# Four transformer blocks in one launch: when the first sequence's value products of attentions 1 and 3 may run

## The chip, the cores and the metric

The kernel runs on one core of a Trainium2 chip. The core has a matrix engine (PE; its weight loads are listed apart as PEld), a vector engine (DVE), a scalar engine (ACT), a general engine (POOL) and an engine that issues transfers (SP). Each engine works through its own list of instructions in the order in which the program wrote them, and waits for the others at semaphores. The metric is the time of one execution on the device in microseconds (us); the quoted time is a median of runs.

## The reference

`reference()` passes `x` (4 sequences of 512 tokens, 288 channels, float32) through four blocks. Each block takes a conditioning vector per sequence, makes six rows of shift, scale and gate from it, and adds an attention and a feed-forward part to `x`:

```
mod = silu(c) @ w_ada + b_ada                       # shift, scale, gate, twice
h   = layernorm(x) * (1 + scale) + shift
q, k, v = split(h @ w_qkv + b_qkv)                  # 16 heads of 18
x   = x + gate * (softmax(q k^T / sqrt(18)) v @ w_proj + b_proj)
h   = layernorm(x) * (1 + scale2) + shift2
x   = x + gate2 * feed_forward(h)                   # 288 -> 1152 -> 288, gelu
```

Blocks 0, 1 and 3 attend over the tokens of a sequence. Block 2 attends, for each token, over its own 16 heads. The feed-forward part of block 0 is a mixture of four experts, two for each token; the other blocks have one plain feed-forward part.

## The kernel before

**Stages.** On the PE, attention 0 comes first, then the experts (19 blocks of 256 rows, `expert_block`), then attention 1. Attention 2 (`attention_over_heads`, a generator called the chain) runs beside the feed-forward part of block 1 and the beginning of that of block 2, whose remainder (`half_mlp`) is followed by attention 3 and its feed-forward part.

**Attention over tokens** (`attention`, called for blocks 0, 1, 3). The work is cut into 16 units: four sequences times four groups of four heads. A unit has four steps, one for each 128 tokens, so there are 64 steps. A step computes two things for the four heads of a unit: in `weights` the scores of its 128 keys and the exponentials of them (ACT, line 750), and in `maxima` the scores of 128 queries of the unit six steps ahead, whose row maxima DVE takes (line 722). `sum_values` multiplies the exponentials with the values, two steps at a time.

**What a unit needs.** `queries_keys(b, m)` computes a packed block of 128 rows of queries and keys (line 640; ACT copies it out at line 666). `spread(u)` then moves the rows of unit `u` by nine transfers (line 702) to their places in a tile `qk`: for each head `j` the queries or keys go to the partitions `32 j` and up, in pieces of at most 19 rows. The first unit of attention 1 sends heads 0 and 1 by SP and heads 2 and 3 by ACT; the first unit of attention 3 sends heads 0 and 1 by SP and heads 2 and 3 by POOL. `values(b, t)` computes the values of 128 tokens: three matrix products (line 640, six records of 288 columns each) and a DVE copy into the tile `va` (line 650).

**Before step 0.** Attentions 1 and 3 are "hidden": the maxima that belong to the steps −6 to −1 are made by `ahead(step, c)` while the PE still works on the feed-forward part before. One `ahead` makes the scores of four heads in two pairs, heads 0 and 1 and then heads 2 and 3 (line 712), and DVE reduces each (line 735). `set_maxima(0)` then turns the maxima of the first unit.

**The order of the work** is fixed when the program is written. The feed-forward functions call `gap(us)` between small groups of matrix products. A gap raises a counter `now` by one and takes work out of the list `products`, which is sorted by due time: the first task in the list whose keys are all marked as ready is taken, **due or not**, as long as the gap's budget is above 0 (0.5 in the experts, 0.3 in `half_mlp`). A value product costs 0.48 for each of its three products, a pair of `ahead` 1.3. After the products, the gap gives the lists of DVE work, of loads and of spreads their turn. `spread` marks its unit as ready two gaps after it was written. So the order rests on a count of gaps; when the data really arrives is a matter of the semaphores alone: an engine that reaches an instruction too early stands still.

While attention 2's chain is alive, a gap closes whatever task it took, that is, it writes it out whole. If a step of the chain wants a bank of PSUM and the gap's products used one, the chain waits for the next gap; in that next gap `products` gets a budget of 0, and the chain comes first.

In the steps, `whole_products(us)` plays the part of the gap: it raises the counter twice, takes ready tasks until their cost passes the budget (0.3 in even steps, 1.7 in odd ones), and beyond it takes those that are due. Even steps put products in the banks 0 to 3, odd ones in 4 to 7, beginning at the first; these are the banks that the scores of the step use too.

The value products are entered so, `s0` being 0 for the first sequence:

```
for t in range(TB):
    free = ("va", l) if b == 0 else ("values free", l, b - 1, t)
    at = s0 + (-1, -1, 1 if b else 0, 1)[t]
    hold = [("step", l, at)] if at >= 0 else [] if l else [("step", l, -2)]
    task(
        products, start - 30 if at < first_step else at_step(at),
        [("ht", l, 0, b), ("loaded", l, 0), free] + hold, values(b, t)
    )
```

A task with `hold` can't be taken before its step is marked. Other due times ahead of step 0 are −50, −48 and −34 for the packed blocks 0 to 2, −20 for block 3, and −24, −21, ... −9 for the six `ahead`.

Of the kernel before, what the change touches and what calls it, by code (L numbers as in the profile page):

```python
# [60 lines left out]
def tile_dit_blocks(ctx: ExitStack, tc: tile.TileContext, x_in, cond_t, sel_den, sel_b, w_gate, layers, out):  # L61
# [52 lines left out]
    def task(where, due, reads, gen):  # L114
        where.append((due, reads, gen))
        where.sort(key=lambda item: item[0])
# [449 lines left out]
    def chunks(l, half, b):  # L566

        key = (l, half, b)
        mod = mods[l, half]
        if half == 0:  # L570
            ht[key] = work.tile([P, NK, S], F32, tag="ht", bufs=2, name=f"ht_{l}_{half}_{b}")
        else:
            ht[key] = work.tile([P, NK, S], F32, tag="hm", bufs=4, name=f"ht_{l}_{half}_{b}")
        for k in range(NK):
            if half == 0:
                at, n = k * KP, KP + (1 if k == NK - 1 else 0)
            else:
                at, n = k * P, P if k < KF else CX - KF * P
            to = other()
            for t in range(TB):  # L580
                nc.tensor.transpose(to[:n, t * P : (t + 1) * P], xh[key][:, t, at : at + n], ident)
            nc.scalar.activation(
                ht[key][:n, k, :], to[:n, :], AF.Identity, bias=mod[:n, 0, k, b : b + 1],
                scale=mod[:n, 1, k, b : b + 1],
            )
            if k == NK - 1:
                held.remove(key)
                mark(("ht",) + key)
            yield Whole(0.43)
# [15 lines left out]
    def attention(l, start):  # L605
# [14 lines left out]
        def at_step(s):  # L620
            return start + 2 * (s - first_step) + 1
# [22 lines left out]
        def values(b, t):  # L644
            pv = other()[:, :C]
            h = ht[l, 0, b]
            yield from product(
                pv, lambda r, k: h[r, k, t * P : (t + 1) * P], lambda r, k: w["wv"][r, k, :], 0.48
            )
            nc.vector.tensor_copy(heads(vas[0])[:, t, :, :HD], pv.rearrange("p (h d) -> p h d", d=HD))  # L650
            mark(("values", l, b, t), 0)
            count(b)
            yield 0.48
# [17 lines left out]
        def straight(u):  # L671

            h, t = ht[l, 0, 0], spreads_of[u]
            qk[u] = t
            for s in range(2):
                pq = other()
                yield from product(pq, lambda r, k: wholes[0][r, u, k, s, :], lambda r, k: h[r, k, :], 0.86)
                nc.scalar.activation(t[:, s, :], pq, AF.Copy)
                count(0)
                if s:  # L680
                    mark(("spread", l, u), 1)
                    if u == direct[-1]:
                        warm = small.tile([P, 1], F32, tag="warm", bufs=1, name=f"warm_{l}")
                        nc.scalar.activation(warm, ident[:, :1], AF.Exp)
                yield Whole(0.86)
# [139 lines left out]
        def project(b, t):  # L825
            pp = other()[:, :C]
            for k in range(NK):
                n = KP + (1 if k == NK - 1 else 0)
                nc.tensor.matmul(  # L829
                    pp, done["turned", b, k][:n, t * P : (t + 1) * P], w["wp"][:n, k, :], start=k == 0, stop=k == NK - 1  # L830
                )
                if k < NK - 1:
                    yield 0.48
            add_gated(b * TB + t, 1, pp.unsqueeze(1), gates[l, 0], f"a_{l}_{b}_{t}")
            if t == TB - 1:
                mark(("x", l, 1, b))
            yield 0.48
# [60 lines left out]
        def ring_of(b, m):  # L898

            m, b = (m - 3, b) if m >= 3 else (m - 3 + NQB, b - 1)  # L900
            if b < 0:
                return None
            return b * NG + min(NG - 1, ((m + 1) * P - 1) // UQ)
# [13 lines left out]
        for b in range(B):  # L917
            s0 = b * NG * TB
            last = s0 + NG * TB
            first = hidden and b == 0  # L920
            task(
                lanes, start - 70 if first else at_step(s0 - LEAD - (9 if l or b > 1 else 12) if b else s0 - LEAD - 6),
                [("x", l, 0, b)] + ([("scattered", B - 1)] if l == 1 else []) + ([("step", l, 0)] if b else []),
                norm(l, 0, b, 10 if first and prev == OVER_HEADS else 3),
            )
            free = [("first products", l, b - 2)] if b >= 2 else []
            if prev == OVER_HEADS and b < 2:

                free = [[("first products", prev, B - 1), ("x", prev, 1, B - 2)], [("x", prev, 1, B - 1), ("first products", l, 0)]][b]
            task(  # L930
                products, start - 60 if first else at_step(s0 - 12 if b else s0 - LEAD - 4),
                [("xh", l, 0, b), ("mod", l, 0)] + free, chunks(l, 0, b),
            )
            for t in range(TB):
                free = ("va", l) if b == 0 else ("values free", l, b - 1, t)
                at = s0 + (-1, -1, 1 if b else 0, 1)[t]
                hold = [("step", l, at)] if at >= 0 else [] if l else [("step", l, -2)]
                task(
                    products, start - 30 if at < first_step else at_step(at),
                    [("ht", l, 0, b), ("loaded", l, 0), free] + hold, values(b, t)  # L940
                )
                at = last + (3, 4, 6, 8)[t] if b + 2 < B else last + (3, 5, 7, 9)[t]
                hold = [("step", l, at)] if b + 1 < B else []
                task(
                    products, at_step(last if b + 1 == B else at),
                    [("turned", l, b, k) for k in range(NK)] + [("gate", l, 0), ("projection", l)] + hold,
                    project(b, t),
                )
            for u in direct if b == 0 else ():
                task(  # L950
                    products, at_step(-LEAD - 2 + 4 * u),
                    [("ht", l, 0, 0), ("whole", l, u)] + ([("step", l, -LEAD)] if u else []), straight(u),
                )
            for m in range(2 if b == 0 and direct else 0, NQB):
                free = [("spread", l, ring_of(b, m))] if ring_of(b, m) is not None else idle
                at = s0 + (((-10, -9, -5, -1, 3) if l else (0, 0, -4, -3, 3)) if b == 0 else (-11, -9, -7, -5, -3))[m]
                hold = [("step", l, at)] if at >= 0 or l == 0 else []
                due = start - (50, 48, 34, 20)[m] if hidden and at < 0 else at_step(at)
                units = range(m * P // UQ, min(NG, -(-(m + 1) * P // UQ)))
                task(  # L960
                    products, due, [("ht", l, 0, b)] + [("loaded", l, g) for g in units] + free + hold,
                    queries_keys(b, m),
                )
            for g in range(NG):
                u, s = b * NG + g, s0 + g * TB
                free = [("qk free", l, u - 4)] if u >= 4 else idle
                blocks = range(g * UQ // P, -(-(g + 1) * UQ // P))
                if u not in direct:
                    task(
                        spreads, start - (42, 32)[u] if hidden and u < 2 else at_step(s - LEAD - 2),  # L970
                        [("packed", l, b, m) for m in blocks] + free + ["cleared"] + ([("set", l, 0)] if direct and u == 2 else []),
                        spread(u),
                    )
                due = start - 9 if hidden and u == 0 else at_step(s + 1 - LEAD + TB - 2) + 1
                task(products, due, [("maxima", l, u)], set_maxima(u))
                at = s + TB + (2 if g < NG - 1 else 1)
                hold = [("step", l, at)] if at < N_STEPS - LEAD else []
                task(products, at_step(at), [("sums", l, u)] + hold, outputs(u))
            for k in range(NK):
                at = s0 + (12, 16, 18)[k]  # L980
                hold = [("step", l, at)] if at < N_STEPS - LEAD else []
                task(products, at_step(at), [("outputs", l, b * NG + g) for g in (k, k + 1)] + hold, turned(b, k))
# [1035 lines left out]
    for l in range(n_layers):  # L2018
# [7 lines left out]
        if l == 0:  # L2026
# [4 lines left out]
            for i, half in enumerate(halves):  # L2031
                free = [("step", 0, 7 * i + 1)] + ([("modulated",) + halves[i - 1]] if i else [])
                at = base + 2 * (LEAD + 7 * i) + 2
# [190 lines left out]
```

## Time and profile before

| | us |
|---|---|
| median of 3 runs (2169.55 to 2182.09) | 2180.47 |
| the profiled execution, its own time | 2180.11 |
| its span, from the first to the last instruction | 2178.4 |
| PE busy | 2056.8 (94%) |
| DVE busy | 1067.0 (49%) |
| ACT busy | 813.6 (37%) |
| POOL busy | 541.3 (25%) |
| mean granted PE clock | 0.975 |
| stages on the PE: step 0 of attention 1 begins at | 836.26 |
| step 0 of attention 3 begins at | 1695.85 |

Times inside the execution count from the start of the span. In a timeline, a line gives the start, the length, the engine (with a q where it issues a transfer), the line of the kernel, the operation, the tiles written and read, their shapes, the number of instructions merged, and in brackets how long the engine had stood idle and who released it. A float32 matrix product appears as two records. The ends of PE records are modelled, so the distance between starts is the better measure. In a table of stretches, each line gives the stretch, its length, the busy time of PE, PEld, DVE, ACT and POOL with the number of instructions, the granted PE clock, the share of the transfer engines and GB/s.

### The profile page before, as it was taken

The numbers are of one execution on the slowest core, as the hardware profiler recorded it, in microseconds if no ns is written. First come the engines' busy times: TensorE is split into PE (matmuls) and PEld (weight loads), VectorE is DVE, ScalarE is ACT, GpSimd is POOL, SyncE is SP. The second block draws the span as 40 slices with busy tenths as digits, with TensorE's granted clock in tenths as the row PEclk, the third lists the DMA queues.
The fourth block names the chain that finished last, engine by engine and source line by source line (L and its number), as shares of the span: only waits on it lengthen the run. The fifth ranks groups of instructions, "written<-read, shape, count | busy, mean of one in ns | idle before, by whom it ended". The sixth has DMA issues, their size and how long they took to land.

```text
span 2178.4 us, 28974 instructions
## 1 busy us (share of the span) xinstructions
PE 2056.8 (94%) x10782; PEld 1156.8 (53%) x10782; DVE 1067.0 (49%) x1656; ACT 813.6 (37%) x1333; POOL 541.3 (25%) x589
## 2 busy tenths in 40 slices
PE   7899999899999998999999999979999999999997
PEld 3334434367777574344354667656767444443554
DVE  4656656532002404576445769699730555664101
ACT  2434444522222123445436332333422555455211
POOL 2212131231004112020011395769711101001101
PEclk9999999999999999999999999979999999999999
DMA  4153222346666353000000000302210100000000
GB/s 95 54 178 119 61 59 37 109 148 195 203 200 199 113 170 93 21 26 17 19 6 20 18 9 16 69 17 30 34 50 18 40 19 18 14 18 1 11 11 22
DMA packets 171832, 139.13 MB, mean 64 GB/s; under 512 B 80694, under 2 KB 153838, under 8 KB 171692
## 3 DMA queue, kind: packets, MB, share of 16 engines
q1 hardware_dynamic: 163370, 123.92, 20.3%
q0 software_dynamic: 8224, 13.20, 2.1%
q8 instruction: 86, 1.41, 0.3%
q14 instruction: 54, 0.44, 0.1%
q10 hardware_dynamic: 98, 0.16, 0.0%
HBM read 96.49 MB, written 26.00 MB: 56 GB/s over the span
## 4 chain that ended last, share of the span: by engine, by line
PE 65%; DVE 14%; POOL 3%; issue 2%; ACT 2%; DMA 1%; SPq 0%; POOLq 0%; DVEq 0%; ACTq 0%
PE banks L712 12%; PE banks L640 8%; PE banks L1739 7%; PE banks L1719 6%; PE banks L778 5%; PE banks L1893 4%; PE banks L1870 4%; PE banks L1952 3%; DVE pq L1021 3%; PE banks L1930 3%; DVE hs L1027 3%; DVE mx L722 3%; PE banks L829 3%; PE banks L1725 2%; POOL pv L1040 1%
## 5 line engine op out<-in xcount | busy, mean ns | idle before, releaser
L722 DVE TENSOR_REDUCE mx<-banks 128x4 f32<-128x2048 f32 (+1 forms) x354 | 423.7, 1238 | 352.7 <-PE banks L712 319.3
L750 ACT ACTIVATE ex<-banks 128x1024 f32<-128x1024 f32 (+1 forms) x471 | 377.6, 865 | 312.1 <-PE banks L712 312.0
L712 PE MATMUL banks<-qk 32*128 32x512 f32 x3072 | 440.4, 627 | 26.6 <-DVE mx L722 7.4
L712 PEld LDWEIGHTS banks<-qk 32*128 32x128 f32 x3072 | 167.8, 185 | 201.3 <-issue 73.1
L1040 POOL TENSOR_TENSOR pv<-hs,qk 128x1152 f32<-128x1152 f32 x60 | 192.5, 3233 | 9.8 <-ACT hs L1194 9.8
L778 PE MATMUL banks<-ex,va 128*32 128x512 f32 x1536 | 191.6, 612 | 2.5 <-ACT ex L750 2.5
L640 PE MATMUL banks<-ht,wqk 96*128 96x512 f32 (+1 forms) x348 | 169.2, 619 | 10.2 <-DVE mx L722 9.7
L1739 PE MATMUL banks<-w_b,hid_b 128*128 128x288 f32 x648 | 175.3, 416 | 0.0
L1719 PE MATMUL banks<-block,w_b 128*128 128x256 f32 (+1 forms) x684 | 159.0, 371 | 0.6 <-ACT hid_b L1731 0.6
L1930 PE MATMUL banks<-ht,w 128*128 128x256 f32 x504 | 133.1, 400 | 21.3 <-ACT hid L1941 21.2
L1952 PE MATMUL banks<-w,hid 128*128 128x288 f32 x504 | 147.5, 429 | 0.0
L1739 PEld LDWEIGHTS banks<-w_b,hid_b 128*128 128x128 f32 x648 | 117.9, 189 | 51.0 <-issue 22.1
L1731 ACT ACTIVATE hid_b<-banks,b_b 128x256 f32<-128x256 f32 (+1 forms) x171 | 66.8, 461 | 198.4 <-PE banks L1725 128.6
L1719 PEld LDWEIGHTS banks<-block,w_b 128*128 128x128 f32 x684 | 122.7, 191 | 26.6 <-issue 8.9
L764 POOL DMA_DIRECT2D qk<-maxima x48 | 29.8, 620 | 381.4 <-ACT maxima L763 381.3
L1930 PEld LDWEIGHTS banks<-ht,w 128*128 128x128 f32 x504 | 98.1, 200 | 44.6 <-ACT hid L1941 24.9
L599 POOL TENSOR_TENSOR x<-x,upd_a 128x288 f32<-128x288 f32 x48 | 38.6, 805 | 315.0 <-DVE upd_a L598 288.5
L640 PEld LDWEIGHTS banks<-ht,wqk 96*128 96x128 f32 (+1 forms) x348 | 61.4, 187 | 102.8 <-issue 57.2
L1952 PEld LDWEIGHTS banks<-w,hid 128*128 128x128 f32 x504 | 91.5, 194 | 45.6 <-issue 26.2
L778 PEld LDWEIGHTS banks<-ex,va 128*32 128x32 f32 x1536 | 40.2, 110 | 139.5 <-issue 71.2
L1941 ACT ACTIVATE hid<-banks,b 128x256 f32<-128x256 f32 x126 | 53.6, 471 | 136.9 <-PE banks L1937 136.8
L1052 DVE TENSOR_REDUCE ho<-pv 128x72 f32<-128x1152 f32 x64 | 85.2, 1337 | 30.6 <-POOL pv L1040 30.6
(244 smaller groups left out, 2458.1 us busy)
## 6 DMA issues: line engine op xcount, KB each, us to landing
w_b<-in_w SPq DMA_DIRECT2D x57, 432.0 KB
w_b<-in_w SPq DMA_DIRECT2D x57, 384.0 KB
qk<-qc SPq DMA_DIRECT2D x270, 38.0 KB
wa<-in_wada SPq DMA_DIRECT2D x24, 288.0 KB
x_mem<-zeros SPq DMA_DIRECT2D x21, 256.0 KB
y_mem<-zeros SPq DMA_DIRECT2D x21, 256.0 KB
block<-x_mem SPq DMA_DIRECT2D x17, 288.0 KB
y_mem<-y_b SPq DMA_DIRECT2D x17, 288.0 KB
```

The source lines that it names most:

```text
L640: nc.tensor.matmul(to, st(rows, k), mv(rows, k), start=k == 0, stop=k == NK - 1)
L712: nc.tensor.matmul(to, qk[u][r, of, c * P : (c + 1) * P], qk[u][r, 1 - of, :], start=True, stop=True)
L722: nc.vector.tensor_reduce(mxs[u % 2][:, j : j + n, c], banks[:, bank + j : bank + j + n, :], AX.X, ALU.max)
L750: nc.scalar.activation(ex[step, j // 2][:, j % 2 : j % 2 + n, :], banks[:, to[j] : to[j] + n, :], AF.Exp, scale=SCALE)
L778: nc.tensor.matmul(to[j * HP : (j + 1) * HP, :], vas[0][:, c, at : at + HP], ex[step, j // 2][:, j % 2, :], start=first, stop=last,)
L1040: engine.tensor_tensor(prod, sc[i][:, hs, :].unsqueeze(2).to_broadcast([P, GH, HD, NH]), qkv[i, 2].rearrange("p h d -> p d h").unsqueeze(1 ...
L1719: nc.tensor.matmul(banks[:, UP + j, cols], w1[:, k, j * P : (j + 1) * P], hx[i][:, k, cols], start=k == 0, stop=False)
L1739: nc.tensor.matmul(banks[:, PY + t, :C], hid[j][:, t * P : (t + 1) * P], w2[:, j, :], start=f == 0, stop=f == NF - 1)
L1870: nc.tensor.matmul(banks[:, 4 + j, :], full[:, k, (f % 3) * P : (f % 3 + 1) * P], h[:, k, :], start=k == 0, stop=False,)
L1893: nc.tensor.matmul(banks[:, t, :C], hf[:, t * P : (t + 1) * P], w["w2"][f // 3][:, f % 3, :], start=f == 0, stop=f == NF - 1,)
L1930: nc.tensor.matmul(banks[:, UP + j, :BT], full[:, k, (f % 3) * P : (f % 3 + 1) * P], h[:, k, s], start=k == 0, stop=False,)
L1952: nc.tensor.matmul(banks[:, PY + t, :C], hf[:, t * P : (t + 1) * P], w["w2"][f // 3][:, f % 3, :], start=False, stop=f == NF - 1,)
```

## The change

One line changes: the step for which each of the four value products is held.

```diff
             for t in range(TB):
                 free = ("va", l) if b == 0 else ("values free", l, b - 1, t)
-                at = s0 + (-1, -1, 1 if b else 0, 1)[t]
+                at = s0 + ((-1, -1, 1, 1) if b else (0, 0, 1, 3) if l else (-1, -1, 0, 1))[t]
                 hold = [("step", l, at)] if at >= 0 else [] if l else [("step", l, -2)]
```

For the later sequences (`b` above 0) and for attention 0 the numbers are the same as before. For the first sequence of attentions 1 and 3 they go from −1, −1, 0, 1 to 0, 0, 1, 3: products 0 and 1, which had no hold and were due 30 counts before step 0, wait for step 0; product 2 moves from step 0 to step 1, and product 3 from step 1 to step 3. No instruction is added or removed.

## The prediction

> **What bounds the kernel.** I read the page first: who is busy, and what the chain that ended last consists of.
>
> ```profile
> span 2178.4 us, 28974 instructions
> PE 2056.8 (94%) x10782; PEld 1156.8 (53%) x10782; DVE 1067.0 (49%) x1656; ACT 813.6 (37%) x1333; POOL 541.3 (25%) x589
> ```
>
> PE is the bound, so I ask, stage by stage, whether it ever stands still where products are taken away or put. The table of stretches:
>
> ```profile
> 718.50:725.00 6.50, 6.50 (x32) 4.60 (x30) 0.46 (x1) 1.78 (x5) 0.00 (x0) 1.00 0.42 143
> 757.00:760.60 3.60, 2.03 (x7) 1.11 (x7) 3.60 (x6) 0.00 (x0) 2.80 (x2) 1.00 0.32 94
> 760.70:764.00 3.30, 3.30 (x12) 2.37 (x11) 0.84 (x2) 0.69 (x2) 0.00 (x0) 0.50 0.47 151
> 846.00:852.80 6.80, 5.67 (x19) 3.21 (x23) 5.41 (x13) 0.43 (x2) 3.44 (x3) 0.50 0.41 136
> 876.80:883.50 6.70, 6.66 (x26) 1.89 (x26) 3.01 (x4) 0.59 (x1) 1.25 (x3) 0.50 0.08 29
> 1560.00:1600.00 40.00, 40.00 (x179) 28.03 (x178) 11.72 (x19) 15.33 (x29) 18.52 (x27) 1.00 0.20 56
> ```
>
> Where products 0 and 1 run now (718 to 726, and 1573 to 1583), PE is busy throughout: a product that leaves gives its time back. Lines 3 to 5 show the price of standing still: each follows a wait of PE (1.57, 3.21 and 2.01 us), and in each the granted clock is 0.50.
>
> Then the order of PE around the products, from the timeline, attention 1 first, attention 3 below, and the transfers of the first unit:
>
> ```profile
> 718.51 0.65 PE L640 MATMUL banks<-wqk,ht 96*128 96x288 f32 x2
> 719.00 1.03 PE L1719 MATMUL banks<-block,w_b 128*128 128x256 f32 x4
> 719.86 1.14 PE L640 MATMUL banks<-wqk,ht 96*128 96x288 f32 x4
> 725.17 1.13 PE L712 MATMUL banks<-qk 32*128 32x512 f32 x4
> 726.22 1.24 PE L1739 MATMUL banks<-w_b,hid_b 128*128 128x288 f32 x4
> ...
> 712.37 5.14 ACTq L702 DMA_DIRECT2D qk<-qc  x5
> ```
>
> ```profile
> 1573.57 1.62 PE L640 MATMUL banks<-wqk,ht 96*128 96x288 f32 x6
> 1575.03 1.03 PE L1930 MATMUL banks<-ht,w 128*128 128x256 f32 x4
> 1575.89 0.60 PE L581 MATMUL banks<-ident,xh 128*128 128x128 f32 x4
> 1579.54 0.60 PE L581 MATMUL banks<-ident,xh 128*96 128x128 f32 x4
> 1580.84 1.62 PE L640 MATMUL banks<-wqk,ht 96*128 96x288 f32 x6
> ...
> 1574.59 11.94 SPq L702 DMA_DIRECT2D qk<-qc  x13
> ```
>
> What matters is what the planner puts into the empty gaps. Both times the next ready task is `ahead`, which reads the unit whose transfers are just being issued. How late such a transfer can be, attention 1 shows at its step 6: nine transfers, the first issued at 862.55, the last at 867.13, and PE stands until 876.84.
>
> ```profile
> 862.55 14.41 SPq L702 DMA_DIRECT2D qk<-qc  x14
> 876.84 2.04 PE L712 MATMUL banks<-qk 32*128 32x512 f32 x2 [2.01 <-DMA qk<-qc]
> ```
>
> So nine transfers took 14.3 us, 1.6 us each, one after the other; the last was usable 9.7 us after its issue.
>
> **The change, part by part.** All against the profiled execution (span 2178.4, 2180.11 in all, 0.4 under the median of 2180.47).
>
> *Out of the feed-forward parts.* A value product takes 1.46 us of PE (1573.57 to 1575.03). Two leave, in each attention: −2.9.
>
> *What takes their gaps, attention 1.* Product 0 took the rest of one gap and all of the next, product 1 the two after. The first unit's spread was written four gaps earlier and is marked. So all six `ahead` and block 3 move three gaps forward. The first pair (heads 0 and 1, sent by SP from 705.43, records of arrival up to 715.2) starts at 718.51 in time, takes 1.05 (725.17 to 726.22), then come 0.86 of line 1719: the second pair starts at 720.4. Head 3's last transfer was issued by ACT at 716.92. Bounds from the rows: 1.6 us later (718.5, no wait) or 9.7 later (726.6, 6.2 of wait). The trace's semaphore records for that transfer end at 724.8, and those of step 6's last one at 876.7, just where PE was released; I take 724.8: +4.4. Afterwards the clock is halved: 1.7 us lost as at 760.7, 2.8 as at 847 to 852.8, 3.4 as at 876.8; I take 2.8, by the nearest wait (3.21).
>
> *A gain.* PE's wait of 1.57 at 758.65 is the last `ahead` behind eight DVE instructions of `combine` (lines 1797, 1798), which are bound to their gap. Three gaps earlier, that pair's reduces stand ahead of `combine` on DVE. The wait and its half clock go: −1.6 − 1.7 = −3.3; 0 if something else waits there. Block 3's spread (nine SP transfers) moves too, ahead of the load of an expert block on SP; 5 us of issuing there are covered by the 20 us until that block is widened.
>
> *Attention 3.* Product 0's gap comes one gap before unit 0 is marked, and nothing in `products` is ready: the chain, which waited one gap for a bank, takes it, and its three transposes (L581) come one gap earlier each. The gap that the third of them had is now free, unit 0 is marked, and the first `ahead` goes in; the second takes product 1's gap. PE gets there at 1579.54 − 1.46 + 0.44 = 1578.5. It needs heads 0 and 1, whose four SP transfers were issued from 1574.59 to 1576.52. Bounds: 1578.1 (no wait) or 1586.2 (7.7). The records say 1579.8, 1581.3, 1582.8 and 1584.4, again 1.5 apart; I take 1584.4: +5.9, and +2.8 of half clock. SP's issue hangs on attention 2's last transfer (L1070 at 1574.06), not on PE, so it doesn't come earlier. Behind the waiting score stand on PE all feed-forward products, and nothing covers them. The last four `ahead` are now in four consecutive gaps together with four DVE statistics (2.5 us), where block 3's 2.6 us of PE lay between them: four times four reduces at 0.6 us and the statistics are 12 us of DVE against 7 of PE, some 5 us of waiting for banks, where the rows at 1604.03 to 1621.78 have 4: +1.0 (0 to 2).
>
> *In the steps.* Step 0 now runs products 0 and 1. Their PE time fills a wait that is there (0.83 us for the reduce, both attentions) but the next `weights` waits for one more DVE copy, 0.45. In attention 1 that copy pushes DVE's line 1797, which at 842.64 takes 1.37 instead of 0.36 while POOL runs, into POOL's end: I count 0. In attention 3 DVE runs without a pause up to the reduce at 1702.84: +0.45. Step 1 has one product as before. Step 3 gets product 3 ahead of block 4: PE is behind there, DVE idles (2.87 us before its next reduce): +1.45 in each. Block 4, its nine transfers and the steps that read them all shift alike, so the wait at 876.84 stays.
>
> Attention 1: −2.9 + 4.4 + 2.8 − 3.3 + 1.45 = +2.5. Attention 3: −2.9 + 5.9 + 2.8 + 1.0 + 0.45 + 1.45 = +8.7. Together +11.2: 2180.1 + 11.2 = **2191**.
>
> *Two rules of the Trainium skill.* "DMA: Bandwidth & Descriptors", section "Why a DMA increments its semaphore by 16 and not by 1", has a transfer of SP or ACT use the largest number of engines up to 16 that divides its rows, so 19 rows go through one engine; at its 27 GiB/s, 38 KB would take an estimated 1.3 us. That speaks against this change as the rows do (1.6), and with it the waits would be about a fifth shorter, some 2 us less in all. "TensorE: Matmul & The Clock Gate", in its table of advice, warns only of idle gaps over about 3 us; the rows show 0.50 after 1.57 and 2.01. By the rule the gain of 1.7 at 760.7 falls away, and the sum is 1.7 higher.
>
> **Rivals.**
> - *The transfers are there in time* (faster). It decides whether heads 3 and 1 have landed by 720.4 and 1578.5; the low bounds (718.5, 1578.1) say yes, the step 6 row says no. Then both waits and both half clocks go: 11.2 − 4.4 − 2.8 − 5.9 − 2.8 = −4.7, 2175.
> - *Only one of the waits happens.* Attention 3's alone: 11.2 − 7.2, 2184; attention 1's alone: 11.2 − 8.7, 2182.5.
> - *Nothing fills the gaps*, the bare trade: −5.8 + 0.45 + 2.9 = −2.5, 2178. Against it: the gaps take ready work, due or not.
> - *Worse.* Waits at the high bounds (+1.8 each), half clocks at 3.4, new waits of the chain's transposes and of DVE: +18 and more, 2200 and over.
>
> **How the numbers follow.** Both waits: 0.72, at 2191, of itself 2183 to 2200 by the bounds of clock and waits. One wait: 0.11. In time: 0.08. Bare trade: 0.03. Worse: 0.06. From 2178 to 2202 I leave out the rival in time and most of the worst, some 0.15. One per cent (21.8 us) is about what a measurement of this kernel can tell from no change: over 2202.3 I give 0.06, under 2158.7 0.01, between 0.93.
>
> **What would show it.** In the changed profile: line 712 with 4.4 us of wait for `qk<-qc` near 725 and 5.9 near 1584, each followed by a clock of 0.50; no wait near 758; line 650 four times in the first steps of each attention and not in the feed-forward parts. Wrong it would be if line 712 ran without a wait there, or if another task than `ahead` stood in the gaps.

## The result and the profile after

| | us |
|---|---|
| kernel before, median of 16 runs (2167.61 to 2187.53) | 2171.97 |
| changed kernel, median of 16 runs (2180.44 to 2193.77) | 2184.87 |
| ratio, 95% interval | 1.005, 1.0033 to 1.0068 |
| profiled execution of the changed kernel, its own time | 2185.94 |
| its span (2178.4 before) | 2184.2 |

The change costs half a per cent: 10.9 us of 2172, between 7.2 and 14.8. The ratio on record is not the quotient of the two medians, which is 1.0059 (12.9 us); here and below, differences in microseconds that are said to be by the ratios are the ratio minus 1, times the median of the kernel before from the same set of runs. PE has as many instructions as before and slightly less busy time.

The page of the changed kernel, the span and the engines:

```profile
span 2184.2 us, 28972 instructions
PE 2053.2 (94%) x10782; PEld 1156.6 (53%) x10782; DVE 1067.2 (49%) x1656; ACT 813.2 (37%) x1333; POOL 541.6 (25%) x589
```

PE was busy for 2056.8 us before. A longer span with less busy time means that PE waits more, so the waits come first. The waits of PE in the changed kernel (waiting line, releaser, total us, number, longest):

```profile
PE banks L712 <- DMA qk<-qc: 11.0, 6, 4.1
...
PE banks L1696 <- DVE block L1678: 3.2, 1, 3.2
```

Before, line 712 waited 6.2 us for these transfers, and line 1696 at no place for line 1678. Now the timeline of the changed kernel. Attention 1 first; it runs some 7.4 us earlier here than in the profile before, because attention 0 was that much shorter in this execution:

```profile
713.93 1.12 PE L712 MATMUL banks<-qk 32*128 32x512 f32 x2
718.02 1.19 PE L712 MATMUL banks<-qk 32*128 32x512 f32 x1 [2.97 <-DMA qk<-qc]
...
762.73 0.42 PE L1696 MATMUL banks<-ident,block 128*96 128x128 f32 x2 [3.16 <-DVE block L1678]
```

Then attention 3:

```profile
1568.13 15.00 SPq L702 DMA_DIRECT2D qk<-qc  x15
...
1569.16 0.60 PE L581 MATMUL banks<-ident,xh 128*96 128x128 f32 x4
...
1574.82 1.09 PE L712 MATMUL banks<-qk 32*128 32x512 f32 x2 [4.08 <-DMA qk<-qc]
...
1577.91 2.40 PE L712 MATMUL banks<-qk 32*128 32x512 f32 x6 [2.00 <-DMA qk<-qc]
...
1616.26 3.26 PE L712 MATMUL banks<-qk 32*128 32x512 f32 x7 [0.66 <-DVE mx L735]
```

The order is the predicted one: `ahead` (line 712) stands where the value products were, and the third transposes (line 581) come a gap earlier. In attention 1 head 2 goes through at 713.93 and head 3 waits 2.97 us. In attention 3 heads 0 and 1 wait 4.08 and 2.00, and a later `ahead` waits 0.66 for DVE. The line at 762.73 wasn't foreseen.

The table of stretches, changed kernel (stretch, length, busy us of PE, PEld, DVE, ACT, POOL with instructions, granted PE clock, DMA share, GB/s):

```profile
715.10:718.00 2.90, 0.00 (x0) 0.01 (x1) 0.68 (x1) 0.00 (x0) 0.00 (x0) 0.65 0.09 31
718.10:733.00 14.90, 14.90 (x32) 6.65 (x33) 3.27 (x5) 1.20 (x3) 0.00 (x0) 0.50 0.22 61
759.60:762.70 3.10, 0.00 (x0) 0.00 (x0) 3.04 (x4) 0.00 (x0) 2.84 (x4) 1.00 0.02 5
763.80:767.10 3.30, 3.30 (x7) 2.43 (x8) 0.00 (x0) 1.20 (x3) 0.27 (x1) 0.50 0.77 220
1576.20:1589.70 13.50, 11.79 (x32) 6.64 (x33) 4.81 (x8) 1.05 (x2) 0.00 (x0) 0.50 0.07 27
1617.10:1623.90 6.80, 6.80 (x23) 3.39 (x21) 3.48 (x6) 3.30 (x7) 0.44 (x2) 0.50 0.52 170
```

The same table for the kernel before, a stretch of the same place and length:

```profile
718.10:733.00 14.90, 14.90 (x63) 8.44 (x62) 4.99 (x9) 2.18 (x6) 0.00 (x0) 1.00 0.41 129
```

This pair is the heart of the case. In both, PE is busy for 14.90 of 14.90 us by its records (whose ends are modelled); before it gets through 63 instructions at a clock of 1.00, now through 32 at 0.50. A wait of 2.97 us is followed by 15 us at half speed. The clock's records give the half-speed periods as 715.97 to 733.04 (17.07 us), 763.76 to 767.17 (3.41), 1576.13 to 1589.78 (13.65) and 1617.09 to 1623.92 (6.83).

To see where time is won and lost without the variation of the other stages, I cut two stretches out of each attention, from the starts in the timelines: the **front**, from the first line-640 product of block 0 to the first line-712 score of step 0, and the **first steps**, from there to the 189th record of line 778 in attention 1 (in step 24) and to the 77th in attention 3 (in step 10). Differences from the profile before, in us, one profiled execution each; the kernels below the second row are those of the experiments:

| kernel | front 1 | steps 1 | front 3 | steps 3 | time to before, interval |
|---|---|---|---|---|---|
| before (lengths) | 136.16 | 136.63 | 133.65 | 56.05 | |
| after | +8.20 | −2.27 | +12.26 | +1.93 | 1.005 (1.0033 to 1.0068) |
| only_att1 | +7.77 | −2.24 | 0.00 | 0.00 | 1.001 (0.9991 to 1.003) |
| only_att3 | +2.50 | +1.13 | +7.95 | +1.96 | 1.0037 (1.0017 to 1.0056) |
| late_ahead | −2.10 | −0.51 | −1.92 | +1.95 | 0.9977 (0.9958 to 0.9997) |
| split_rows | −4.86 | −2.21 | +6.21 | +1.95 | 0.9982 (0.9964 to 1.0001) |
| busy_instead | +1.46 | −2.09 | +6.93 | +1.94 | 1.002 (0.9998 to 1.0041) |
| later_2_3 | +1.35 | −1.50 | 0.00 | +1.79 | 1.000 (0.9979 to 1.002) |
| att1_split | −2.94 | −1.33 | 0.00 | 0.00 | 0.9975 (0.9958 to 0.9992) |
| att1_split_combine | −7.94 | −0.97 | 0.00 | −0.01 | 0.9953 (0.9937 to 0.9969) |
| before_combine | −4.62 | −0.90 | −0.01 | 0.00 | 0.9966 (0.9951 to 0.9981) |

Attention 3 repeats to 0.01 us wherever its order is unchanged. Attention 1 doesn't: with the order of before, front 1 took 136.16, 137.51 and 138.67 us in three executions and steps 1 took 136.63 and 137.76, with periods of half clock of different length. Its rows are good to about 2 us. The changed kernel's parts sum to +20.1, more than the 5.8 by which the two profiled executions differ: outside these stretches its execution was 14 us shorter, 7.4 of that ahead of any changed instruction. The clock accounts for about that much: ahead of attention 1's front and from the end of its steps to attention 3's front, the profile before was at 0.50 for 81.9 us in all and the changed kernel for 51.2, and half of the difference is 15 us. So the periods of half clock vary between executions, in stages that the change doesn't touch too.

### The profile page after: what moved, and what is told of

The parts are those of the page before. It is cut to its first block, busy times and chain, and to the rows that moved or that the text cites. A ratio compares the mean times of both kernels' runs of the same rounds, so it can differ in the third digit from the quotient of the medians.

```text
span 2184.2 us, 28972 instructions
## 1 busy us (share of the span) xinstructions
PE 2053.2 (94%) x10782; PEld 1156.6 (53%) x10782; DVE 1067.2 (49%) x1656; ACT 813.2 (37%) x1333; POOL 541.6 (25%) x589
## 4 chain that ended last, share of the span: by engine, by line
PE 64%; DVE 13%; POOL 4%; issue 3%; ACT 2%; DMA 1%; SPq 0%; POOLq 0%; ACTq 0%; DVEq 0%
PE banks L712 12%; PE banks L640 8%; PE banks L1739 7%; PE banks L1719 6%; PE banks L778 5%; PE banks L1893 4%; PE banks L1870 4%; PE banks L1952 3%; PE banks L1930 3%; DVE mx L722 3%; DVE pq L1021 3%; PE banks L829 3%; DVE hs L1027 2%; POOL pv L1040 2%; PE banks L1725 1%
## 5 line engine op out<-in xcount | busy, mean ns | idle before, releaser
L1739 PE MATMUL banks<-w_b,hid_b 128*128 128x288 f32 x648 | 180.3, 425 | 0.0
```

The lines of the kernel that those rows point to most:

```text
L1739: nc.tensor.matmul(banks[:, PY + t, :C], hid[j][:, t * P : (t + 1) * P], w2[:, j, :], start=f == 0, stop=f == NF - 1)
```

## Experiments

**Each attention alone.** The hold of one attention is changed, the other keeps the old steps.

```diff
-                at = s0 + ((-1, -1, 1, 1) if b else (0, 0, 1, 3) if l else (-1, -1, 0, 1))[t]
+                at = s0 + ((-1, -1, 1, 1) if b else (0, 0, 1, 3) if l == 1 else (-1, -1, 0, 1))[t]
```

> The new steps 0, 0, 1, 3 in attention 1 alone; attention 3 keeps the old ones. Theory (the waits for the first unit's transfers, with the half clock after them, are what the change costs): line 712 waits some 3 us near 715 to 718, the clock is 0.50 for over 10 us after it, no wait of line 712 near 1575. By the prediction's sum +2.5 us; by the stage marks of the two profiles +6 (8 lost ahead of step 0, 2 gained in the steps): 2174.5 to 2178 against 2172 of the kernel before. Rival (the products cost more in the steps than in the feed-forward part): the same total, but the loss lies behind step 0, after 836 us, and the stretch from 715 to 765 is not longer.

With `l == 3` in its place:

> The new steps in attention 3 alone. Theory: line 712 waits 6 us near 1575 to 1584 in two parts, the clock is 0.50 for about 13 us after it, nothing else is new: by the prediction's sum +8.7, by the stage marks of the two profiles +6 (2178 to 2181). Rival (the cost is in the steps): the loss lies behind 1696 us. If the two halves of the change hinder each other, the two shares do not add up to the whole's +13.

Measured: 2183.13 (ratio 1.001) and 2186.64 (1.0037), against 2175.67 of the kernel before. In microseconds by the ratios: +2.2 (−2.0 to +6.5) and +8.0 (+3.7 to +12.2), together 10.2 beside the +10.9 of the whole change. By the medians alone it would be +7.5 and +11.0, so attention 1's share is not well known. In the profiles each attention shows its own waits for the first unit's transfers and not the other's. Attention 1 alone, timeline:

```profile
718.21 1.19 PE L712 MATMUL banks<-qk 32*128 32x512 f32 x1 [3.04 <-DMA qk<-qc]
...
762.23 0.42 PE L1696 MATMUL banks<-ident,block 128*96 128x128 f32 x2 [3.17 <-DVE block L1678]
```

Attention 3 alone, timeline:

```profile
1588.89 1.09 PE L712 MATMUL banks<-qk 32*128 32x512 f32 x2 [2.74 <-DMA qk<-qc]
1591.98 2.40 PE L712 MATMUL banks<-qk 32*128 32x512 f32 x6 [2.00 <-DMA qk<-qc]
```

The loss lies ahead of step 0 in both: front 1 is 7.8 us longer in the one, front 3 is 8.0 longer in the other. The rival that puts the cost into the steps fails in attention 1, whose steps are shorter, and holds for 2 of the microseconds in attention 3. The second wait of 2.00 us is the same as in the changed kernel; the first is 2.74 instead of 4.08, and the half clock behind it 6.83 us instead of 13.65. The shorter wait comes from an earlier issue: SP sends the first of the four transfers of heads 0 and 1 12.4 us after the start of front 3 here, as in the kernel before, and 13.9 us in the changed kernel (1568.13, where front 3 starts at 1554.25). In the profiles with attention 3's old order this ranges from 11.5 to 14.0 us, so the change doesn't set it.

**`ahead` kept where it was.** Units 0 and 1 are marked as ready later, so that nothing fills the freed gaps.

```diff
-            mark(("spread", l, u), 2)
+            mark(("spread", l, u), {1: 9, 3: 13}.get(l, 2) if u < 2 else 2)
```

> The changed kernel, but units 0 and 1 of attentions 1 and 3 are marked as ready later (9 counts after the spread in attention 1, 13 in attention 3, instead of 2), so that the first `ahead` stands about where it stood before the change and nothing fills the freed gaps. Theory: the waits for qk<-qc ahead of step 0 go, with their half clock; what is left is the bare trade, -2.5 us against the kernel before: 2169.5 (2166 to 2174). Rival (the cost is the products in the steps): the time stays near that of the changed kernel, 2182 to 2186.

Measured: 2174.38, ratio 0.9977: by the ratio 5 us faster than before (0.7 to 9.1; the medians differ by 1.3 only) and 16 below the changed kernel. Both waits for `qk<-qc` are gone, and the clock is 1.00 where they were. Stretches of that kernel:

```profile
709.80:725.00 15.20, 15.20 (x68) 10.00 (x68) 0.76 (x1) 4.33 (x10) 0.00 (x0) 1.00 0.39 114
1566.00:1590.00 24.00, 24.00 (x111) 17.36 (x110) 3.18 (x4) 11.27 (x23) 6.30 (x10) 1.00 0.27 77
```

So the products in the steps are not what the change pays for. The rival that nothing fills the gaps, with its −2.5, is what this kernel is, and the time agrees with it; the four parts in its profile sum to −2.6. The old wait of the last `ahead` is there again, 1.54 us at 753.44.

**Faster transfers.** The order of the PE is that of the changed kernel, but the transfers of 17 and 19 rows that SP and ACT issue for unit 0 are cut in two.

```diff
-                        queue.dma_start(t[to : to + n, s, :], packed[b, m][r : r + n, :])
+                        for i, k in ((0, min(n, 16)), (16, n - 16)) if u == 0 and l and queue is not nc.gpsimd else ((0, n),):
+                            if k > 0:
+                                queue.dma_start(t[to + i : to + i + k, s, :], packed[b, m][r + i : r + i + k, :])
```

> The changed kernel, but the transfers of 17 and 19 rows that SP and ACT issue for unit 0 of attentions 1 and 3 are cut into one of 16 rows and one of the remaining 1 or 3. Order of the PE as in the changed kernel. Theory (the wait is for transfers that go row after row at 1.55 us each): the 16-row pieces land much faster, the wait near 718 goes, that near 1575 falls from 6.1 to under 3 us (more issues, and the transfers of attention 2 ahead of them), and the time falls to 2168 to 2176. Rival (transfers wait for something else, the issue or the receipt, not for their rows): twice the issues make the waits longer, 3 to 4 us each more, 2188 and over.

Measured: 2175.71, ratio 0.9982, by the ratios 15 us below the changed kernel. In this kernel the lines behind the cut stand two further down, so line 712 is 714. Its timeline in attention 3, and stretches at both places:

```profile
1567.15 13.74 SPq L704 DMA_DIRECT2D qk<-qc  x19
...
1571.90 1.12 PE L714 MATMUL banks<-qk 32*128 32x512 f32 x2
...
1573.87 2.15 PE L714 MATMUL banks<-qk 32*128 32x512 f32 x6 [0.85 <-DMA qk<-qc]
```

```profile
709.00:725.00 16.00, 16.00 (x69) 9.50 (x70) 3.34 (x5) 4.43 (x10) 0.00 (x0) 1.00 0.41 122
...
1574.60:1584.70 10.10, 10.10 (x29) 5.23 (x25) 4.37 (x7) 1.05 (x2) 0.00 (x0) 0.50 0.09 28
1612.10:1618.90 6.80, 6.80 (x20) 4.02 (x22) 3.78 (x7) 3.24 (x7) 0.79 (x3) 0.50 0.59 193
```

Twice the transfers, and they are sooner there: heads 0 and 1 of attention 3 are complete 6.7 us after the first issue (1567.15 to 1573.87), against 9.8 in the changed kernel (1568.13 to 1577.91). In attention 1 the wait is gone altogether, and front 1 is 13 us shorter than in the changed kernel. The rival (issue, not rows) falls. Not all of the shorter wait in attention 3 is owed to the cut: SP's first issue is 2.2 us earlier in this execution (11.7 us after the start of front 3, against 13.9), and the cut itself brings the other 3.1. Attention 3 shows something that the theory didn't say: the wait falls from 6.08 to 0.85 us, and front 3 is still 6.2 us longer than before: even after 0.85 us the clock is halved for 10.24 us, and for 6.83 us again at 1612.

**Work in the place of the waits.** This separates the waiting from the clock.

```diff
                 pair = [other() for _ in range(2)]
+                if step == -LEAD and j == {1: 2, 3: 0}[l]:
+                    for _ in range({1: 14, 3: 28}[l]):
+                        nc.tensor.matmul(pair[0][:, :P], ident, ones, start=True, stop=True)
```

> The changed kernel with useless PE work at the two places where it waits for transfers: 14 products of 128 columns (some 3.0 us at the full clock) ahead of the second pair of the first `ahead` of attention 1, 28 (some 6.0 us) ahead of the first pair in attention 3. Nothing else differs, and the transfers land when they land. Theory (the half clock after the waits is the larger part of the price: 17.07 and 13.65 us of 0.50 in the changed kernel's profile, some 8.5 and 6.8 us lost, against 3.0 and 6.1 us of waiting): the work takes the place of the waits, the clock stays at 1.00, and the kernel gets faster by the added work, 8 to 15 us below the changed kernel: 2170 to 2177, ratio to before 0.998 to 1.001. Rival (the waits themselves are the price and the clock costs little behind them): the time stays within 3 us of the changed kernel's, ratio 1.004 to 1.007. If the dummies stand in the wrong place, both a wait and the work show: 1.008 and over.

Measured: 2178.86, ratio 1.002 against 1.005 of the changed kernel, 6.5 us less; the intervals just overlap (0.9998 to 1.0041 and 1.0033 to 1.0068). That lies between the two forecasts (8 to 15 us, and at most 3), so the times alone lean to the theory and don't prove it. The profile shows the clock. Stretches:

```profile
712.30:730.00 17.70, 17.70 (x89) 10.99 (x88) 4.78 (x9) 2.15 (x5) 0.00 (x0) 1.00 0.24 75
...
1567.30:1573.60 6.30, 6.30 (x58) 6.18 (x56) 0.00 (x0) 0.00 (x0) 0.00 (x0) 1.00 0.10 31
1573.60:1587.30 13.70, 13.70 (x68) 9.20 (x68) 4.88 (x8) 3.46 (x7) 0.00 (x0) 1.00 0.06 23
1609.50:1616.20 6.70, 6.70 (x22) 2.88 (x17) 3.12 (x6) 3.30 (x7) 0.00 (x0) 0.50 0.36 109
```

PE multiplies ones by the identity for 3.3 us and 6.4 us, for nothing, and then goes on at 1.00. Front 1 is 6.7 us shorter than in the changed kernel and front 3 is 5.3 shorter, although PE spends slightly longer at these places than it waited there. Where a wait is left, behind the last `ahead` of attention 3 (0.66 us), the half clock of 6.83 us is left too.

With that, front 3 can be summed: 2.9 us less for the two products, plus the waits (or the work in their place, and the 0.66 us behind a later `ahead`), plus half of the time at half clock. A period of half clock is counted from where PE goes on, so that the wait inside it isn't counted twice.

| kernel | products | waits or work | half of the half-clock time | sum | measured |
|---|---|---|---|---|---|
| after | −2.9 | 6.74 | (11.87 + 6.83) / 2 = 9.35 | 13.2 | 12.26 |
| only_att3 | −2.9 | 5.40 | (5.59 + 6.83) / 2 = 6.21 | 8.7 | 7.95 |
| split_rows | −2.9 | 1.51 | (10.24 + 6.83) / 2 = 8.54 | 7.1 | 6.21 |
| busy_instead | −2.9 | 7.1 | 6.83 / 2 = 3.41 | 7.6 | 6.93 |
| late_ahead | −2.9 | 0.66 | 0 | −2.2 | −1.92 |

Five kernels within 1 us: the waits and the clock are the account of front 3, and the clock is the larger item in three of them.

**Only products 2 and 3 later.**

```diff
-                at = s0 + ((-1, -1, 1, 1) if b else (0, 0, 1, 3) if l else (-1, -1, 0, 1))[t]
+                at = s0 + ((-1, -1, 1, 1) if b else (-1, -1, 1, 3) if l else (-1, -1, 0, 1))[t]
```

> Holds -1, -1, 1, 3 instead of 0, 0, 1, 3: products 0 and 1 stay ahead of step 0 as in the kernel before, only product 2 goes from step 0 to 1 and product 3 from 1 to 3. So the front of both attentions is that of before, and only the steps differ. By the prediction's terms step 3 costs 1.45 in each attention and the wait for qk<-qc near 877 stays: +2.9, 2175 to 2178 against some 2173 to 2175 of the kernel before. By the stage marks of the profiles (first steps of attention 1 2.2 us shorter in all kernels with the new steps, no half clock near 877; attention 3 1.5 longer): -1, and no wait of line 712 for qk<-qc near 877. If the gain of attention 1's steps hangs on products 0 and 1 in step 0, the wait and the half clock near 877 are there again.

Measured: 2173.84 against 2174.28, ratio 1.000 (0.9979 to 1.002): undecided by time. By the profile steps 3 cost +1.79, beside +1.95 of the full change. In both, 1.5 of it arises in step 3 of attention 3, from its score to that of step 4, where product 3 now stands; ahead of step 3 they are 0.3 and 0.5 us behind the kernel before. Steps 1 are 1.5 shorter, as in the other kernels with the new steps. Its timelines, step 0 of attention 3 and the place of the old wait near 877 in attention 1:

```profile
1696.85 3.48 PE L712 MATMUL banks<-qk 32*128 32x512 f32 x16 [2.48 <-DVE mx L722]
```

```profile
881.91 1.09 PE L712 MATMUL banks<-qk 32*128 32x512 f32 x2 [1.89 <-DMA qk<-qc]
```

Without a product in step 0, PE waits 2.48 us for the reduce there, where it waited 0.83 beside product 2: a product in step 0 is free. The wait for `qk<-qc` is there too (1.89). So is it in `att1_split`, `att1_split_combine` and `busy_instead` (1.87 to 1.93), which have all the new steps of attention 1. In the changed kernel, `only_att1`, `late_ahead` and `split_rows`, a wait of 2.40 to 2.99 us for DVE stands some 6 us earlier in its place. With the old steps it is the same: 2.01 us for the transfers in the kernel before and in `before_combine`, 1.07 for DVE, some 6 us earlier, in `only_att3`. One and the same order shows the one or the other, so neither is the change's doing.

**The wait at line 1696.** `combine` of sequence 1 is bound to a gap; here it comes six gaps later. Twice: on top of attention 1's new steps with the cut transfers, and on the kernel before.

```diff
-        mark(("outs", b), 24)
+        mark(("outs", b), 30 if b == 1 else 24)
```

The base of the first, only_att1 with the cut of `split_rows`:

> The new steps in attention 1 alone, with the transfers of unit 0 cut into 16 rows and the rest. Theory (waits for single-engine transfers and the half clock after them cost all that the change lost): ahead of step 0 some 5 us are gained, in the first steps 2, attention 3 is as before: -7, ratio 0.997 (2165 to 2169 against 2173). Rival (the split only trades one wait for another): ratio 1.000 or more.

And with `combine` later:

> As att1_split, and `combine` of sequence 1 becomes ready 30 counts after its gather instead of 24, so that its eight DVE instructions come after the widening of block 16 (line 1678), not ahead of it. Theory (the prediction's gain of 3.3 did not come because the same DVE work now holds up the widening, and line 1696 waits 3.2 us for it instead of the last `ahead` 1.6): that wait goes, 3 to 5 us less than att1_split, ratio 0.995 to 0.996 against before. Rival (something else is just as late there, the load of the block): the wait stays, released by a DMA, and the time is that of att1_split.

The kernel before with `combine` later:

> The kernel before with only that later `combine` (30 instead of 24). Theory: the wait of 1.57 us near 758.6 (line 712 behind DVE's lines 1797 and 1798) goes, and with it the half clock of 3.4 us after it: -3.3, ratio 0.9985. Rival (`combine` costs the same wherever it stands, since it holds DVE for 6 us and another reader waits): 1.000.

Measured: 2167.12 (0.9975), 2163.70 (0.9953) and 2165.04 (0.9966), against 2174.28. The last is 7.4 us less than before by the ratio (4.1 to 10.7), more than the 3.3 of the forecast. The wait is not traded for another. The stretch of `att1_split_combine` that holds the place (line 1698 there):

```profile
757.00:775.00 18.00, 18.00 (x91) 13.62 (x90) 6.75 (x12) 3.79 (x10) 6.42 (x5) 1.00 0.57 173
```

PE runs through at 1.00. Front 1 is 5.0 us shorter than in `att1_split`, for 3.17 us of wait and half of 3.41 us of half clock; in the kernel before the later `combine` brings 4.6, for 1.57 and half of 3.41, which is 1.3 more than the two account for. Part of the rest may be the clock: in `only_att3` and `later_2_3`, where the last `ahead` waits equally long (1.57 and 1.56), the half clock after it lasted 6.83 us. `att1_split_combine` has the lowest median of the set: by the ratio 10.2 us under the kernel before (6.7 to 13.7) and some 21 under the changed kernel. Its interval overlaps that of `before_combine`, so whether the new steps and the cut transfers add to the later `combine` is not shown.

## Why the prediction was right, and where its steps were not

The sum of +11.2 (0.51%) met +10.9 (0.50%). The shares agree with the ratios too, +2.5 for attention 1 (2.2 by the runs) and +8.7 for attention 3 (8.0), but these are known to some 4 us only. In the profiles the terms are partly of other sizes and cancel. What was right is the mechanism: `ahead` fills the freed gaps, PE waits for the first unit's transfers, and the clock is halved after it.

- **What fills the gaps: right.** `ahead` and the transposes stand where they were foreseen. `late_ahead` shows that this alone turns −5 us into +10.9 (by the ratios).
- **Attention 1, second pair waits 4.4: right in kind, 2.97 to 3.04 in size.** I took the pair as one. From its start to the release pass 4.09 us (713.93 to 718.02), but head 2 goes first and fills 1.1 of them; only head 3's product waits.
- **Attention 3, heads 0 and 1 wait 5.9: right in kind, its size met by luck.** `only_att3` has SP's issue where my rows had it, and there the wait is 4.74 us: again I took the pair as one, and head 0's score fills 1.1 of the time. In the changed kernel SP issued 1.5 us later, which makes 6.08. That SP's issue doesn't come earlier was foreseen; that it moves by 2.5 us from one execution to another was not. That the transfers go row after row was read from the 1.5 us between them, and `split_rows` bears it out. The 1.6 us by way of "nine transfers in 14.3 us" was a misreading: from 862.55 to 867.13 eight are issued, one of them of a single row. The rule in "DMA: Bandwidth & Descriptors", section "Why a DMA increments its semaphore by 16 and not by 1" (19 rows, one engine; 16 rows, sixteen), is what that cut was made by; the runs agree with it in time, and none of them shows the engines themselves.
- **Half clock of 2.8 after each wait: the mis-sized term.** The rows that I took it from showed periods of 3.41 and 6.83 us; after the new waits they lasted 17.07 and 13.65, of which some 7.5 and 6 us are lost once PE runs again. That is 7 to 8 us more than I allowed for both. With one attention changed they were 13.65 in attention 1 (6.8 lost) and 6.83 in attention 3, where 2.8 us are lost, just what I had taken.
- **Attention 1's gain of 3.3 at 758.65: wrong.** I asked who stands behind `combine` on DVE and moved the last `ahead` out of its way. I didn't ask who is next there. It is the widening of block 16 (line 1678), and line 1696 needs it: 3.16 us of wait instead of 1.57. The step named its own exception ("0 if something else waits there"), and even that was too good. That the same DVE work was behind both waits is shown by `before_combine` and `att1_split_combine`, where one line takes either away.
- **DVE's queue behind the last four `ahead`, +1.0 (0 to 2): low.** The wait is 0.66 us, but each profile that has it behind a line-712 score (the changed kernel, `only_att3`, `split_rows`, `busy_instead`) shows 6.83 us of half clock with it, 3.4 us lost.
- **Steps of attention 3, +0.45 and +1.45: right.** +1.93 to +1.96 in five kernels. In the changed kernel 0.46 of it is there ahead of step 3, and step 3 adds 1.49.
- **Steps of attention 1, +1.45: wrong in sum.** Seven kernels with the new steps took 0.5 to 2.3 us less than the profile before, `later_2_3` 1.5 less; the old steps themselves varied by 2 us (−0.90 to +1.13). So no cost is left at the end of the stretch. Product 3 does cost in step 3: from its score to that of step 4 pass 7.19 us in the changed kernel and 5.70 before. But the clock was at 0.50 for 13.66 us of these steps in the profile before and in `only_att3`, for 10.24 in `before_combine`, and for only 3.41 to 10.24 with the new steps; the changed kernel's 10.2 us less are worth some 5. Whether the new steps bring that about or it fell out so stays open.
- **The wait at 876.84 stays: right in part.** With the new steps a wait of 1.87 to 2.99 us is there in every kernel, but in four of them it stands some 6 us earlier and DVE releases it.
- **The rivals.** The transfers in time is excluded by the waits. The bare trade was built as `late_ahead`: it is about what would have happened if the unit's ready mark had meant arrival.

The front of attention 1 came out at +8 in the two profiles where I had +1.0, and its steps at −2.3 where I had +1.45; attention 3's front at +8 and +12 where I had +6.8. That the totals agree is owed in part to this cancelling, and to the profiled executions not being the median ones: `only_att1` has +5.5 in its profile and +2.2 by its runs.

## What to carry to other kernels

Price a wait of the matrix engine at its length plus half of the slow period that follows, and don't take that period from the nearest wait: here it lasted from nothing to 17 us after waits of 0.66 to 4 us, and equal waits had different ones. Where a change frees a gap, find out what the planner puts there and whether its ready mark means that the data has arrived or only that its transfer was written; and where a wait vanishes, name the next reader of the engine that caused it. Try cutting transfers whose number of rows is awkward: here, 16 rows and a rest in place of 17 and 19 rows took 15 us off the changed kernel (by the ratios), although there were twice as many to issue.

## What the runs showed that I had not expected

- **A long half clock under full load.** PE was busy for 14.90 of 14.90 us and stayed at 0.50 (718.10 to 733.00). All periods but the one that ends each trace lasted 3.41, 6.83, 10.24, 13.65, 17.07 or 20.48 us, multiples of 3.41. "TensorE: Matmul & The Clock Gate", section "Part 1: The HAM clock gate", gives a window of 3413 ns, which agrees. It has the full clock come back after at least one busy window of sustained work; in this row, taken as its records stand, more than four such windows were not enough.
- **The length doesn't follow from the wait.** After 0.85 us of waiting in `split_rows` came 10.24 us. After 1.57 us at the last `ahead` of attention 1 came 3.41 us in the kernel before and 6.83 in `only_att3`. After the wait of 3.16 or 3.17 us at line 1696 came 3.41 us (the changed kernel, `only_att1`, `att1_split`), 6.83 (`busy_instead`) or none (`split_rows`). After about 0.66 us there were 6.83 us in four kernels and none in `late_ahead`. What decides it stays open.
- **Useless work made the fronts shorter than waiting did.** With 9.7 us of products of ones in the place of 9.05 us of waits, the two fronts were 12.1 us shorter in the profile, and the kernel 6.5 us faster by the ratios, whose intervals just overlap.
- **An idle DVE with nothing to show for it.** In the changed kernel the reduce of step 4's scores starts at 868.89, 7.80 us after DVE's last work, though PE's records of those scores end at 864.95; PE then waits 2.99 us for it. The profile names PE's line 581 as the releaser, whose records end at 868.25; what held the reduce for the rest isn't shown.
